# Later gathers, later output copies and no early matmuls in a four-layer routed transformer kernel

## The chip, the core and the metric

The kernel runs on one core of one Trainium2 chip. The metric is the device time of one launch in microseconds (us). The kernel before takes 969.09 us, the median of three runs (968.87 to 969.17).

## The reference

The input `x` holds 64 sequences of 64 tokens with 512 features, in float32. Four layers are added to it one after the other. Each sequence has its own indices, known only when the kernel runs.

```python
x = x + (einsum('bsi,bio->bso', x, W0[id]) + b0[id])           # id: one of 16 experts per sequence
x = x + (x @ W1.T + scale[a] * (x @ A[a].T) @ B[a].T)          # a: one of 7 adapters, rank 16
x = x + attention(x)                                            # 8 query heads, 4 key/value heads of 64
x = x + (einsum('bct,bcd->bdt', x, W3[subject]) + b3[subject])  # one of 8 matrices, 64 x 64
```

The attention layer makes q, k and v, normalises q and k, rotates them by their positions, writes k and v into a cache of blocks of 16 positions that a table of 257 entries per sequence addresses, and lets each token see the last 256 positions. So a sequence needs up to 255 old rows of the cache and its own 64 new ones, 320 positions in all.

## The kernel before, in words

A tile is 128 tokens, two sequences; there are 32 tiles. `x` lies transposed on the host (features on the partitions), so that the first matmul needs no transpose. All matmuls are in float32. The order of the instructions on every engine is written out by hand (`manual_schedule`): what is emitted first runs first on its engine, and the framework adds the semaphores.

**First part (0 to about 540 us): layers 0 and 1, and q, k, v.** Tiles go in groups of 1, 1, 2 and then seven times 4. For each group `layer1` does the matmuls of layer 1 (`pxa` L650, `p` L665, the adapter's L673), and while the next group's tiles come up, one turn of the loop does for tile `i0` of the next group and tile `i` of this one: `layer0(i0)` (L275, eight matmuls with two expert matrices that a DMA of 1 MB each brings), `load_next` (the loads two tiles ahead), `other` (index arithmetic on VectorE, copies of old cache rows), `turn_x2(i)` (four transposes L684), a q product and a k/v product (`product`, L140, four matmuls each), `turn0(i0)` (four transposes L298, then the addition L299 on VectorE), and `keep_kv(i)` (normalisation and rotation of k, then a store to the DRAM buffer `kvd`). When a group is followed by one twice as large (groups 1 to 2 and 2 to 4), each tile `i` has two turns, `half` 0 and 1, and its k/v product stands ahead of `turn0(i0)` in the second; in the groups of four it stands behind, inside the call of `keep_kv`. At the very start, two small helpers run matmuls of the identity with itself: `warm(3)` and `warm(6)` (L222), around the four matmuls `pb` that turn the biases.

**Second part (about 540 to 968 us): attention and layer 3, a loop of 32 steps.** Step `s` emits in this order:

- `load_kv(s + 2)`: five indirect DMAs (L801) on GpSimd's queue, 128 rows of 2 KB each, from `kvd` into the tile `kv` (four buffers, so tile `s + 2` takes the buffer of `s - 2`, which `attend(s - 2)` in step `s - 1` read last). In steps 0 and 1 a one-element copy on GpSimd, `after_keys`, holds them until the keys are turned. `load_mask(s + 2)` and `load_q(s + 2)` go to SP's queue.
- `scores(s)`: eight matmuls `ps` L874, one per key/value head and sequence; for each a fused add-and-maximum on VectorE (L882) and an exponential on ScalarE (L886) that also sums the row.
- `add_one(s - 2)`: an addition on GpSimd to layer 3's matrix (L847). `load_pair(s - 1)` goes to SP's queue.
- `attend(s - 1)`: 24 matmuls `po` L921 on the keys' values; then VectorE copies both results, `oT` L939.
- `normalise(s, 0)` and `normalise(s, 1)`: for each half a reciprocal L894 and four scalings L898 on VectorE.
- `last(s - 4)` in even steps from 4 on: layer 3 (`pz` L961), and the store of the output.
- `project(s - 2)`: eight records of `py` L949, then the addition L953 on VectorE.
- `keys(s + 1)`: ten transposes `pkt` (L855, L861), copied by ScalarE (L856, L862).
- `turn(s)`: 20 transposes `ppt` (L907, L911) of the normalised rows, copied to `pT` by VectorE and ScalarE in turn (L908, L912).

In steps 0 to 3 the q rows of the last tiles are still rotated on VectorE between these (`parts`). PSUM has eight banks. One belongs to `py`; the other seven are a ring, in which every new bank takes that of the seventh before it: `ppt` takes banks of `ps` and `po`, and `ps` takes those of `pkt` and `ppt`, once the copies have emptied them.

Of the kernel before, what the change touches and what calls it, by code (L numbers as in the profile page):

```python
# [12 lines left out]
F32 = mybir.dt.float32  # L13
I32 = mybir.dt.int32
AF = mybir.ActivationFunctionType
ALU = mybir.AluOpType
# [9 lines left out]
H, G, HD = 8, 4, 64  # L26
# [24 lines left out]
NT = NTOK // 128  # L51
# [8 lines left out]
def body(ctx: ExitStack, tc: tile.TileContext, a: dict, out: bass.AP):  # L60
    nc = tc.nc
    V, S, P, TE = nc.vector, nc.scalar, nc.gpsimd, nc.tensor
# [14 lines left out]
    ident = const.tile([128, 128], F32, name="ident")  # L77
# [21 lines left out]
    def bank(name):  # L99
        return ring.tile([128, 512], F32, tag="ring", name=name)  # L100
# [36 lines left out]
    def product(i, w, name, pool=None):  # L137
        ps = pool.tile([128, 512], F32, name="py") if pool else bank(name)
        for c in range(KC):
            TE.matmul(ps, x2s[i][:, c, :], w[:, c, :], start=c == 0, stop=c == KC - 1)  # L140
        return ps
# [43 lines left out]
    with ExitStack() as pa:  # L185
# [29 lines left out]
                ptok[h * B : (h + 1) * B, 4 * B : 4 * B + 1], tokf[:, 3, :], one[:, :1], start=True, stop=True  # L215
            )

        def warm(n):

            pw = bank("pw")  # L220
            for _ in range(n):
                TE.matmul(pw[:, :128], ident, ident, start=True, stop=True)  # L222

        toki = ptok[:, : 4 * B].rearrange("p (k b) -> p k b", k=4)

        warm(3)
        takes = su.tile([E, B], F32, name="takes")
        V.tensor_scalar(takes, toki[:E, 0, :], pidxf[:E], None, ALU.is_equal)
        biasT = su.tile([128, KC, B], F32, name="biasT")
# [1 line left out]
        for c in range(KC):  # L231
            TE.matmul(pb[:, c * B : (c + 1) * B], btab[:, c * 128 : (c + 1) * 128], takes, start=True, stop=True)
        V.tensor_copy(biasT.rearrange("p c b -> p (c b)"), pb[:, : KC * B])
        warm(6)
        kvi = su.tile([128, 1], I32, name="kvi")
        V.tensor_copy(kvi, ptok[:, 4 * B : 4 * B + 1])

# [65 lines left out]
        wkv = wts.tile([128, KC, D], F32, name="wkv")  # L303
# [384 lines left out]
        def keep_kv(i, pk, X):  # L688
            kvn = wk.tile([128, 2 * G * HD], F32, name="kvn", bufs=2)
            to = kvn[:, : G * HD].rearrange("p (h d) -> p h d", d=HD)  # L690
            run(turned(pk, G, to, wk, X, 1, *gains(1, i, wk, P)))
            S.copy(kvn[:, G * HD :], pk[:, G * HD :])
            nc.sync.dma_start(kvd[OLD + i * 128 : OLD + (i + 1) * 128], kvn)
# [38 lines left out]
        for g in range(NG - 1):  # L732
            layer1(tiles[g])
            if g == 0:
                scalars()
                turns[0] = rotation(0)
                for _ in range(4):
                    next(turns[0])
            elif g == 1:
                far()  # L740
            n, m = len(tiles[g]), len(tiles[g + 1])
            for k in range(m):

                i0, i, half, halves = tiles[g + 1][k], tiles[g][k * n // m], k % (m // n), m // n
                layer0(i0)
                load_next(i0)
                other(i0)
                if i0 % 4 == 1 and i0 // 4 + 1 < NT // 4:
                    load_a(i0 // 4 + 1)
                    load_b(i0 // 4 + 1)  # L750
                q = asked.pop() if asked and half == 0 else None
                if half == 0:
                    turn_x2(i)
                if q is not None:
                    pq = product(q, wq, "pq")
                pk = product(i, wkv, "pk") if half else None
                turn0(i0)
                if g == 0:
                    run(turns[0])
                    next(bg)  # L760
                    next(bg)
                if q is not None:
                    run(parts_q(q, pq, P))
                    made.append(q)
                if half == halves - 1:
                    keep_kv(i, pk if half else product(i, wkv, "pk"), P)
                    if i < NT - LATE:
                        asked.append(i)
                    if len(made) > 1:
                        turn_q(made.pop(0))  # L770
        layer1(tiles[-1])
        i = NT - LATE
# [19 lines left out]
    kvp = ctx.enter_context(tc.tile_pool(name="kvp", bufs=4))  # L792
    bp = ctx.enter_context(tc.tile_pool(name="bp", bufs=2))

    kvs, kTs, mbs, prs, pTs, oTs, qTs, pairs, x3s = {}, {}, {}, {}, {}, {}, {}, {}, {}

    def load_kv(i):
        kv = kvs[i] = kvp.tile([128, 5, 2 * G * HD], F32, name="kv")
        for n in range(5):
            at = idxn[:, n % 2, 2 * i + n // 2 :][:, :1] if n < 4 else idxh[:, i : i + 1]  # L800
            P.indirect_dma_start(  # L801
                out=kv[:, n, :], out_offset=None, in_=kvd,
                in_offset=bass.IndirectOffsetOnAxis(ap=at, axis=0),
            )

    def after_keys(i):

        seen = bp.tile([1, 1], F32, name="seen")
        P.tensor_copy(seen, kTs[i][0:1, 0, 0:1])

    def load_q(i, queue=nc.sync):
        qT = qTs[i] = bp.tile([128, 2, 2, 2, T], F32, name="qT", bufs=4)
# [51 lines left out]
    def scores(i):  # L864
        kT, mb, qT = kTs.pop(i), mbs.pop(i), qTs.pop(i)
        pr = bp.tile([128, G, 2 * NPOS], F32, name="pr")
        mx = bp.tile([128, G, 2], F32, name="mx")
        sm = bp.tile([128, G, 2], F32, name="sm")
        for gp in range(2):
            for b2 in range(2):  # L870
                ps = [bank("ps") for _ in range(2)]
                for g2 in range(2):
                    rows = slice(g2 * 64, (g2 + 1) * 64)
                    TE.matmul(  # L874
                        ps[g2][:, :NPOS], qT[rows, gp, b2].rearrange("p h t -> p (h t)"),
                        kT[rows, gp, b2 * NPOS : (b2 + 1) * NPOS], start=True, stop=True,
                    )

                for g2 in range(2):
                    g = 2 * gp + g2  # L880
                    p = pr[:, g, b2 * NPOS : (b2 + 1) * NPOS]
                    V.tensor_tensor_reduce(  # L882
                        out=p, in0=ps[g2][:, :NPOS], in1=mb[:, b2, :], scale=-1.0, scalar=3.0e38,
                        op0=ALU.add, op1=ALU.min, accum_out=mx[:, g, b2 : b2 + 1],
                    )
                    S.activation(  # L886
                        p, p, AF.Exp, bias=mx[:, g, b2 : b2 + 1], scale=-1.0, accum_out=sm[:, g, b2 : b2 + 1],
                    )
        prs[i] = (pr, sm)

# [23 lines left out]
    def attend(i):  # L914
        kv, pT = kvs.pop(i), pTs.pop(i)
        oT = oTs[i] = bp.tile([128, KC, 2, T], F32, name="oT")
        po = [bank("po") for _ in range(2)]

        def product(b2, g, rows, n, c, m, start, stop):
            gp, g2 = divmod(g, 2)  # L920
            TE.matmul(  # L921
                po[b2][g2 * 64 : (g2 + 1) * 64, gp * 128 : (gp + 1) * 128],
                kv[rows, n, (G + g) * HD : (G + g + 1) * HD], pT[rows, c, m * 128 : (m + 1) * 128],
                start=start, stop=stop,
            )

        for b2 in range(2):
            for gp in range(2):
                for c in range(2):
                    for g in (2 * gp, 2 * gp + 1):  # L930
                        n = 2 * b2 + c

                        product(b2, g, slice(0, 128), n, g, n, gp == 0 and c == 0, False)
        for gp in range(2):
            for b2 in range(2):
                for g in (2 * gp, 2 * gp + 1):
                    product(b2, g, slice(b2 * 64, (b2 + 1) * 64), 4, G, g, False, gp == 1)
        for b2 in range(2):
            V.tensor_copy(oT[:, :, b2, :], po[b2][:, :256].rearrange("p (k t) -> p k t", t=T))  # L939

# [67 lines left out]
    for s in range(NT):  # L1008
        if s + 2 < NT:
            if s < 2:  # L1010
                after_keys(s)
            load_kv(s + 2)
            load_mask(s + 2)
        if s and s + 2 < NT:
            load_q(s + 2)
        scores(s)
        if s >= 2:
            add_one(s - 2)
        if s:
            load_pair(s - 1)  # L1020
            attend(s - 1)
        else:

            parts[NT - 1] = parts_q(NT - 1, product(NT - 1, wq, "pq", pyp), V, cs[NT - 1])
            turn_q(NT - 3, bp)
        if s == 2:
            next(parts[NT - 1])
        normalise(s, 0)
        normalise(s, 1)
        if s % 2 == 0 and s >= 4:  # L1030
            last(s - 4)
        if s >= 2:
            project(s - 2)
        if s + 1 < NT:
            keys(s + 1)
        if s in (4, 5):
            turn_q(NT - 6 + s, bp)
        elif s in (2, 3):

            run(parts.pop(NT - 4 + s))  # L1040
        turn(s)
        if s == 0:
            load_q(2)
            nc.sync.dma_start(wo, a["woT"].rearrange("(c p) f -> p c f", p=128))
        elif s == 1:
            next(parts[NT - 1])
# [2 lines left out]
    add_one(i - 1)  # L1049
    add_one(i)  # L1050
    project(i - 1, ring=True)
    attend(i)
    last(i - 3)
    last_one(i - 1, 1)
    project(i, ring=True, parts=2)
# [54 lines left out]
```

## Time and profile before

| | us |
|---|---|
| median of three runs | 969.09 |
| the profiled run, device time | 969.89 |
| its span, first to last instruction | 967.9 |
| TensorE busy (PE) | 937.1, 97% |
| VectorE busy (DVE) | 609.0, 63% |
| ScalarE (ACT), GpSimd (POOL) busy | 405.0 and 402.6, 42% each |
| PE busy in 540 to 565, 565 to 578, 578 to 603 | 22.16, 9.20, 24.40 |
| PE busy in 603 to 910, 910 to 968 | 299.14, 54.39 |
| idle of GpSimd ahead of L801, waiting for `po` L921 | 155.8 |
| idle of VectorE ahead of `pT` L908, waiting for `ppt` L907 | 36.4 |

How to read it: the profile is that of one execution. Lines are those of the kernel before; PE is TensorE's matmuls and PEld its weight loads, which run beside them. A matmul's end is modelled, so a matmul that waits for a result can count as busy. The chain of waits goes back from the last instruction to what released it, step by step; a piece named PE is time in which TensorE's own work set the end. In the timeline the bracket at a row's end tells how long its engine stood idle before it and what ended that.

### The profile page before, as it was taken

The numbers are of one execution on the slowest core, as the hardware profiler recorded it, in microseconds if no ns is written. First come the engines' busy times: TensorE is split into PE (matmuls) and PEld (weight loads), VectorE is DVE, ScalarE is ACT, GpSimd is POOL, SyncE is SP. The second block draws the span as 40 slices with busy tenths as digits, with TensorE's granted clock in tenths as the row PEclk, the third lists the DMA queues.
The fourth block names the chain that finished last, engine by engine and source line by source line (L and its number), as shares of the span: only waits on it lengthen the run. The fifth ranks groups of instructions, "written<-read, shape, count | busy, mean of one in ns | idle before, by whom it ended". The sixth has DMA issues, their size and how long they took to land.

```text
span 967.9 us, 17834 instructions
## 1 busy us (share of the span) xinstructions
PE 937.1 (97%) x5425; PEld 513.4 (53%) x5425; DVE 609.0 (63%) x1734; ACT 405.0 (42%) x1081; POOL 402.6 (42%) x604
## 2 busy tenths in 40 slices
PE   8989999999999999999899979999999999999998
PEld 4434444444444444443344546766666666666665
DVE  4744776866976476442216868666767776667673
ACT  1312122322223222233223656656666666666663
POOL 4234355554553544534425543334444333334400
PEclk9989999999999999999999989999999999999999
DMA  8888999999999999999954774766666565666621
GB/s 303 301 291 293 397 397 332 374 375 367 381 335 389 401 339 385 354 362 380 350 217 142 237 254 135 213 206 204 205 197 194 182 193 180 201 197 201 200 68 45
DMA packets 132944, 260.74 MB, mean 269 GB/s; under 512 B 32481, under 2 KB 41186, under 8 KB 132850
## 3 DMA queue, kind: packets, MB, share of 16 engines
q1 hardware_dynamic: 108722, 178.74, 51.3%
q0 software_dynamic: 23232, 79.71, 24.8%
q10 hardware_dynamic: 896, 1.16, 0.3%
q8 instruction: 43, 0.70, 0.3%
q14 instruction: 51, 0.42, 0.1%
HBM read 190.06 MB, written 69.50 MB: 268 GB/s over the span
## 4 chain that ended last, share of the span: by engine, by line
PE 90%; DMA 4%; DVE 3%; SPq 1%; issue 1%; ACT 1%; DVEq 0%; ACTq 0%
PE py L949 12%; PE p L665 11%; PE pq L140 11%; PE p L275 10%; PE pk L140 10%; PE po L921 8%; PE ps L874 8%; PE ppt L907 6%; DMA w<-in_W 3%; PE pkt L855 2%; PE ppt L911 2%; PE px L684 1%; PE pkt L861 1%; PE pqt L174 1%; PE pz L961 1%; PE pt L298 1%
## 5 line engine op out<-in xcount | busy, mean ns | idle before, releaser
L801 POOL DMA_INDIRECT kv<-kvd,idxn x128 | 126.5, 988 | 212.8 <-PE po L921 155.8
L886 ACT ACTIVATE pr<-pr,mx 128x320 f32<-128x320 f32 x256 | 140.1, 550 | 7.2 <-DVE mx L882 3.2
L275 PE MATMUL p<-w,xt 128*64 128x512 f32 x512 | 120.4, 601 | 2.7 <-DMA w<-in_W 2.7
L949 PE MATMUL py<-wo,oT 128*128 128x512 f32 (+1 forms) x264 | 118.3, 591 | 1.7 <-DVE qn L128 1.7
L155 POOL DMA_INDIRECT st<-in_kvc,cidx x68 | 65.9, 970 | 125.1 <-DMA kvd<-st 107.8
L140 PE MATMUL pk<-wkv,x 128*128 128x512 f32 x256 | 115.6, 596 | 0.6 <-ACT x L686 0.6
L665 PE MATMUL p<-w,x 128*128 128x512 f32 x256 | 114.4, 603 | 0.0
L882 DVE CUSTOM_DVE_ANT_0 pr<-ps,mb 128x320 f32<-128x320 f32 x256 | 107.8, 485 | 6.2 <-PE ps L874 4.4
L140 PE MATMUL pq<-wq,x 128*128 128x512 f32 x248 | 111.3, 593 | 0.0
L874 PE MATMUL ps<-kT,qT 64*128 64x320 f32 x512 | 87.3, 460 | 10.8 <-DVE pT L908 6.8
L908 DVE COPY pT<-ppt 128x512 f32<-128x512 f32 x64 | 41.9, 687 | 74.3 <-PE ppt L907 36.4
L133 DVE TENSOR_TENSOR sq<-qn,sg 128x256 f32<-128x256 f32 (+1 forms) x128 | 40.1, 354 | 75.4 <-POOL sg L110 73.5
L898 DVE TENSOR_SCALAR pr<-pr,sm 128x320 f32<-128x320 f32 x256 | 85.2, 394 | 2.2
L921 PE MATMUL po<-pT,kv 128*64 128x128 f32 (+1 forms) x1536 | 84.3, 281 | 1.3 <-issue 1.3
L921 PEld LDWEIGHTS po<-pT,kv 128*64 128x64 f32 (+1 forms) x1536 | 70.5, 137 | 22.0 <-DVE mx L882 14.0
L123 ACT ACTIVATE ss<-ss,epst 128x4 f32<-128x4 f32 (+1 forms) x64 | 19.1, 299 | 146.7 <-DVE ss L122 136.5
L949 PEld LDWEIGHTS py<-wo,oT 128*128 128x128 f32 x264 | 47.5, 189 | 61.5 <-issue 58.4
L665 PEld LDWEIGHTS p<-w,x 128*128 128x128 f32 x256 | 48.3, 193 | 59.0 <-issue 57.2
L140 PEld LDWEIGHTS pk<-wkv,x 128*128 128x128 f32 x256 | 46.3, 190 | 51.1 <-issue 49.8
L275 PEld LDWEIGHTS p<-w,xt 128*64 128x64 f32 x512 | 35.3, 137 | 71.5 <-issue 64.8
L135 POOL TENSOR_TENSOR qr<-qn,sq 128x512 f32<-128x512 f32 x25 | 31.8, 1273 | 90.2 <-DVE qn L134 60.8
L140 PEld LDWEIGHTS pq<-wq,x 128*128 128x128 f32 x248 | 44.9, 190 | 46.2 <-issue 46.2
(202 smaller groups left out, 1336.5 us busy)
## 6 DMA issues: line engine op xcount, KB each, us to landing
w<-in_W SPq DMA_DIRECT2D x62, 1024.0 KB
kvd<-st SPq DMA_DIRECT2D x68, 512.0 KB
xt<-in_xT SPq DMA_DIRECT2D x32, 256.0 KB
x2d<-x2n SPq DMA_DIRECT2D x32, 256.0 KB
kvd<-kvn SPq DMA_DIRECT2D x32, 256.0 KB
qTd<-qTs SPq DMA_DIRECT2D x32, 256.0 KB
qT<-qTd SPq DMA_DIRECT2D x32, 256.0 KB
x2r<-x2d SPq DMA_DIRECT2D x32, 256.0 KB
```

Source lines behind the costliest of these rows:

```text
L140: TE.matmul(ps, x2s[i][:, c, :], w[:, c, :], start=c == 0, stop=c == KC - 1)
L155: P.indirect_dma_start(out=st, out_offset=None, in_=a["kvc"].rearrange("(n r) d -> n (r d)", r=2), in_offset=bass.IndirectOffsetOnAxis(ap= ...
L275: TE.matmul(p0[hs, :], xs[i][:, c, hs], w0s[i][h][:, c, :], start=c == 0, stop=c == KC - 1)
L665: TE.matmul(p1[i], x1s[i][:, c, :], w1[:, c, :], start=c == 0, stop=False)
L801: P.indirect_dma_start(out=kv[:, n, :], out_offset=None, in_=kvd, in_offset=bass.IndirectOffsetOnAxis(ap=at, axis=0),)
L874: TE.matmul(ps[g2][:, :NPOS], qT[rows, gp, b2].rearrange("p h t -> p (h t)"), kT[rows, gp, b2 * NPOS : (b2 + 1) * NPOS], start=True, stop= ...
L882: V.tensor_tensor_reduce(out=p, in0=ps[g2][:, :NPOS], in1=mb[:, b2, :], scale=-1.0, scalar=3.0e38, op0=ALU.add, op1=ALU.min, accum_out=mx[ ...
L886: S.activation(p, p, AF.Exp, bias=mx[:, g, b2 : b2 + 1], scale=-1.0, accum_out=sm[:, g, b2 : b2 + 1],)
L898: V.tensor_scalar(p, p, sm[:, g, b2 : b2 + 1], None, ALU.mult)
L907: TE.transpose(pt[:, n * 128 : (n + 1) * 128], pr[:, g, at : at + 128], ident)
L921: TE.matmul(po[b2][g2 * 64 : (g2 + 1) * 64, gp * 128 : (gp + 1) * 128], kv[rows, n, (G + g) * HD : (G + g + 1) * HD], pT[rows, c, m * 128 ...
L949: TE.matmul(py[:, fs], oT[:, c].rearrange("p b t -> p (b t)"), wo[:, c, fs], start=c == 0, stop=c == KC - 1,)
```

## The change

Four edits. `warm` and both its calls go. The k/v product of a tile moves behind `turn0` in the last turn of the two short groups (`k == m - 1`). In steps 2 to 29 `load_kv(s + 2)` moves behind `scores(s)`, and a one-element copy on GpSimd, `after_scores`, makes it wait for the fourth of the step's eight maxima; for that the maxima lie in two tiles, one for each half of the heads. And the copies `oT` leave `attend` for a function of their own, `keep_outputs`, which the loop calls behind `normalise`.

```diff
-        def warm(n):
-
-            pw = bank("pw")
-            for _ in range(n):
-                TE.matmul(pw[:, :128], ident, ident, start=True, stop=True)
...
-        warm(3)
...
-        warm(6)
...
-                pk = product(i, wkv, "pk") if half else None
+                pk = product(i, wkv, "pk") if half and k < m - 1 else None
                 turn0(i0)
...
-                    keep_kv(i, pk if half else product(i, wkv, "pk"), P)
+                    keep_kv(i, pk if half and k < m - 1 else product(i, wkv, "pk"), P)
...
+    def after_scores(i):
+
+        seen = bp.tile([1, 1], F32, name="seen")
+        P.tensor_copy(seen, mxs[i][0][0:1, 1, 1:2])
...
-        mx = bp.tile([128, G, 2], F32, name="mx")
+        mxs[i] = [bp.tile([128, 2, 2], F32, name=f"mx{gp}") for gp in range(2)]
...
-                        op0=ALU.add, op1=ALU.min, accum_out=mx[:, g, b2 : b2 + 1],
+                        op0=ALU.add, op1=ALU.min, accum_out=mxs[i][gp][:, g2, b2 : b2 + 1],
...
+        return oT, po
+
+    def keep_outputs(oT, po):
         for b2 in range(2):
             V.tensor_copy(oT[:, :, b2, :], po[b2][:, :256].rearrange("p (k t) -> p k t", t=T))
...
         if s + 2 < NT:
             if s < 2:
                 after_keys(s)
-            load_kv(s + 2)
+                load_kv(s + 2)
             load_mask(s + 2)
         if s and s + 2 < NT:
             load_q(s + 2)
         scores(s)
+        if 2 <= s < NT - 2:
+            after_scores(s)
+            load_kv(s + 2)
         if s >= 2:
             add_one(s - 2)
         if s:
             load_pair(s - 1)
-            attend(s - 1)
+            outs = attend(s - 1)
...
         normalise(s, 0)
         normalise(s, 1)
+        if s:
+            keep_outputs(*outs)
         if s % 2 == 0 and s >= 4:
             last(s - 4)
...
-    attend(i)
+    keep_outputs(*attend(i))
```

More of the change, by code (lines that the diff above doesn't have):

```diff
@@ L793, in body @@
     bp = ctx.enter_context(tc.tile_pool(name="bp", bufs=2))
-    kvs, kTs, mbs, prs, pTs, oTs, qTs, pairs, x3s = {}, {}, {}, {}, {}, {}, {}, {}, {}
+    kvs, kTs, mbs, prs, mxs, pTs, oTs, qTs, pairs, x3s = {}, {}, {}, {}, {}, {}, {}, {}, {}, {}
     def load_kv(i):
@@ L883, in scores @@
                         out=p, in0=ps[g2][:, :NPOS], in1=mb[:, b2, :], scale=-1.0, scalar=3.0e38,
-                        op0=ALU.add, op1=ALU.min, accum_out=mx[:, g, b2 : b2 + 1],
+                        op0=ALU.add, op1=ALU.min, accum_out=mxs[i][gp][:, g2, b2 : b2 + 1],
                     )
                     S.activation(
-                        p, p, AF.Exp, bias=mx[:, g, b2 : b2 + 1], scale=-1.0, accum_out=sm[:, g, b2 : b2 + 1],
+                        p, p, AF.Exp, bias=mxs[i][gp][:, g2, b2 : b2 + 1], scale=-1.0, accum_out=sm[:, g, b2 : b2 + 1],
                     )
```

## The prediction

> **What bounds the kernel now.** I read the page's busy times and chain first, then the chain of waits by stretches, then the timeline where the chain leaves TensorE.
>
> ```profile
> PE 937.1 (97%) x5425; PEld 513.4 (53%) x5425; DVE 609.0 (63%) x1734; ACT 405.0 (42%) x1081; POOL 402.6 (42%) x604
> PE 90%; DMA 4%; DVE 3%; SPq 1%; issue 1%; ACT 1%; DVEq 0%; ACTq 0%
> ```
>
> TensorE sets the time. A gain can come only from its holes and from matmuls counted busy while they wait. So I look for what one step of the second part costs with and without a hole. Chain of waits at 705 to 733 us (start, length, what), from the end of step 13 into step 14:
>
> ```profile
> 722.72 1.75 PE ppt L907 x16
> 724.47 0.99 PE ppt L911 x4
> 725.45 0.02 issue
> 725.48 0.70 DVE pT L908
> 726.18 0.04 issue
> 726.22 1.94 PE ps L874 x12
> ```
>
> The same chain at 905 to 950 us, end of step 29; no gather is left to issue there:
>
> ```profile
> 926.46 1.75 PE ppt L907 x16
> 928.21 0.44 PE ppt L911 x4
> 928.65 2.35 PE ps L874 x16
> ```
>
> Without the gathers the score matmuls follow the transposes at once. With them TensorE waits for the copy pT, which frees its PSUM banks. The timeline tells why the copy is late:
>
> ```profile
> 722.55 1.91 PE L907 MATMUL ppt<-ident,pr 128*128 128x128 f32 x16
> 723.49 0.94 POOL L801 DMA_INDIRECT kv<-kvd,idxh  x1 [0.31 <-issue]
> 725.48 1.29 DVE L908 COPY pT<-ppt 128x512 f32<-128x512 f32 x2 [3.12 <-PE ppt L911]
> ...
> 926.30 1.91 PE L907 MATMUL ppt<-ident,pr 128*128 128x128 f32 x16
> 926.94 0.69 DVE L908 COPY pT<-ppt 128x512 f32<-128x512 f32 x1 [0.84 <-PE ppt L907]
> ```
>
> The first four transposes of step 13 were done at 723.15, and VectorE stood idle until 725.48, 1.05 us after the fifth gather left GpSimd (723.49 + 0.94 = 724.43). In step 12 it is 1.08 us (711.73, 712.81), in step 27 1.03 us (915.53, 916.56); in step 29, without gathers, the copy starts 0.04 us after the fourth transpose. So TensorE's reports to VectorE and ScalarE are held back, from about 1.7 us before the fifth gather's end (L862 on ScalarE still started on time at 722.79) until some 1.05 us after it. Reports of VectorE to ScalarE and TensorE are not (L882 to L886 takes 0.04 us in such a stretch at 557).
>
> Price: L949 starts at 602.64 in step 4 and 909.96 in step 28, 307.32 us for 24 steps. The clean pair, 921.74 to 946.11, takes 24.37. Twelve such and two extra q transposes (0.44 each, steps 4 and 5) make 293.3. **14.0 us** are lost to this wait.
>
> The start of the second part has the second hole (chain, 500 to 605 us):
>
> ```profile
> 564.51 2.91 PE ps L874 x8
> 567.43 0.02 issue
> 567.45 0.59 ACT pT L908
> 568.04 0.04 issue
> 568.09 3.55 PE ps L874 x8
> 571.64 3.99 PE po L921 x48
> 575.63 0.02 issue
> 575.65 0.76 DVE oT L939 x2
> ```
>
> Here the fifth gather of kv(4) ends at 566.32; pT comes at 567.39, again 1.07 later. The granted clock is 0.50 from 567.8 to 574.7, and L949 waits for oT and qn until 577.29.
>
> **Part by part.**
>
> *Gathers after the fourth maximum.* Step 13 counts from its first score matmul, 713.05; its transposes L907 begin at +9.67 and the first bank is full at +10.1. Today the five gathers start when attend of that step ends: +5.3 to +11.4, reports free at +12.4. After: the fourth maximum is read at 715.73, +2.7; the small copy on GpSimd adds 0.34 (after_keys: 551.43 to 551.77), so gathers run from +3.1 to +9.2 (6.1 us as today) and reports are free at +10.25. That is just as the first bank fills, so pT is not late. What now falls into the held stretch (+7.5 to +10.25) is the end of L949 (+8.6) and of the key transposes (+8.9 to +9.7). If they all come at +10.25: L953 0.69, then both pT copies 1.29, end +12.3, and the next scores need the first at +12.5. ScalarE: three key copies 1.45, end +11.7, needed at +11.86; its three pT copies end at +13.3, needed at +13.6. No wait. Even steps have pz (0.86) ahead, so everything falls 0.86 later and outside. Behind the waiting copy on GpSimd stand the gathers and add_one; kv(s+2) is wanted by keys in the next step, 8 us after its last gather has landed (+12 or so), and add_one's w3 a step later: nobody waits. On SP nothing moves. Bounds: all 14.0 back, or a leftover of 0.3 per odd step (the spread of the release, up to 1.49 after the fifth gather). I take 1.0 left over: **-13.0**.
>
> *Outputs behind the normalisation.* L939, 0.76 us, waits 0.65 for po in each step; L894 and L898 go ahead of it by up to 1.3 us, held by the last exponential (+6.1). They end near +7.7 instead of +8.7, before L907 (+9.67) in either order. In odd steps the third and fourth ppt take po's banks and now need oT, done at +8.4: hidden. Alone worth 0 in a regular step, without gathers held too.
>
> *Steps 1 to 3.* kv(4) moves to step 2, kv(3) stays. Step 1: last maximum 560.1, eight L898 with two L894 2.9 to 563.0, oT to 563.6; ppt three and four wait for oT, so ppt ends at 564.6 (today 564.5). pT on both engines ends at 565.45 instead of 568.5; then ScalarE's sq 0.62, VectorE's L122 0.69, and the first L882 starts at 566.75 instead of 569.66. From there to the end of po: 4.1 us at full clock (1.58 as in step 3 and 2.50), 570.8; today 6.0. L949 needs qn after the eight L882 (3.3) and 0.9: 571.05 instead of 577.29. Step 2: L949 ends 574.7, kv(4)'s gathers end at 574.9, so L953 starts at 576.0; from it the first L882 of step 3 follows 4.0 later as today (581.03 to 585.04): 580.0 against 585.04. Step 3 has the same rotary work behind L953, may lose 0.6 or win 0.8. **-5.0**; -3.1 if the clock halves again, -5.8 if L953 isn't held.
>
> *No early matmuls.* Nine 128x128 matmuls of 0.42 go. The first weights are there at 6.5, and L275 starts only at 10.16 behind those matmuls; it can now start near 6.5, and its last part waits for the load of 11.98 (today it ends at 14.43). The end of the first part is not earlier for it: tile 1's weights land at 23.04 (chain: 14.14, 8.90 us of DMA), and TensorE waits for them today. The array works at half rate in this trace until about 11.7 (weight loads of L275 0.62 us apart, then 0.43). If it now stayed there until 22, L665 (3.6, from 17.0) and L673 would end near 24.1: +1.0. Between 0 and +1 I take **0**, the row of the DMA. [...]
>
> *Short groups.* Two products L140 (3.6 us each) move behind the four transposes L298: tiles 1 and 3. At 53.87 TensorE idles 3.56 us for L299, but VectorE is busy without a break from 45.96 (rotary work, then a run of L498 that stands ahead of L299), so TensorE's order changes nothing there. At the second place at most 0.3 idle: **0** (-0.3 to 0.1).
>
> Sum -18.0. The profiled run took 969.89 (span 967.9), so 951.9; the median of the runs is 0.8 lower: **951.1**.
>
> **Rivals.**
> 1. *A leftover in each odd step* (14%): the held stretch is longer in its new place and the key copies of ScalarE come late. Each 0.1 us costs 0.1 in twelve odd steps; with 0.5: 957.
> 2. *The delay doesn't come from the gathers* (7%): it stays with pT wherever they run. For it: mask, q and w3 loads also end with step 27. Against: the 1.03 to 1.08 above. Only the 1.7 us of 575.63 to 577.29 is won: 967.4, on the edge of what a measurement of this kernel tells from no change (0.2%, 1.9 us).
> 3. *Slower* (8%): gathers stretch where they now run, beside eight L882 and L898. The release moves with the fifth's end; key copies end 1.5 after it. With 1.4 us more in all an odd and its even step lose 1.6 and the gain of 18 is gone; with 2 us it is 975. The row: the third gather, beside L898, takes 1.08 instead of 0.95, so 0.13 each at most, 0.65 in all. [...]
> 4. *More* (5%): L953 isn't held, and the first part gains too: 947.
>
> **How the numbers follow.** The forecast has 66%, 948.5 to 954. The range leaves out the slower case and the unchanged delay: 947.5 to 961. Faster by over 0.2%: 66, 14, 5 and half of rival 2, 88%; within 4%; slower 8%.
>
> **What would show it.** Chain: 0.4 instead of 0.99 for L911 before each even step, no pT piece; L949 of steps 12 and 14 some 24.4 apart instead of 25.4. L801 starts 3 us after the first score matmul. L949 of step 2 starts 6 us earlier, without the half clock. Wrong if pT still starts 1 us after the fifth gather but with TensorE waiting, or if key copies end after the last transpose.

## The result, and the profile after

The changed kernel takes **974.56 us** (median of six runs, 973.11 to 978.15), the kernel before beside it 969.13 (968.81 to 970.87): a ratio of 1.0059 (95% interval 1.0037 to 1.0081). It is slower by 0.6%, where 951.1 was forecast. The profiled execution took 973.11 us, its span is 971.3. First the page of the changed kernel, busy times and chain:

```profile
PE 931.9 (96%) x5407; PEld 511.7 (53%) x5407; DVE 614.8 (63%) x1734; ACT 402.9 (41%) x1081; POOL 405.4 (42%) x632
PE 88%; DMA 3%; DVE 3%; issue 3%; SPq 2%; ACT 1%; another core or an unknown queue 0%; ACTq 0%; DVEq 0%
```

TensorE is busy 5.2 us less, and yet the span is 3.4 us longer: "issue", time for which the profile shows no cause, went from 1% of the chain to 3%. By stretches, cut where py L949 of a step starts (the first two columns are the profiled executions of before and after):

| stretch | before | after | difference |
|---|---|---|---|
| first part, up to the q product of tile 31 | 545.65 | 539.91 | -5.74 |
| start of the second part, to py of step 4 | 56.92 | 53.47 | -3.45 |
| 24 steps, py of step 4 to py of step 28 | 307.32 | 317.76 | +10.44 |
| from there to the end | 57.99 | 60.19 | +2.20 |

The 24 steps were to get 13 us shorter and got 10 longer. The last row has the same cause, since the gathers now run one step longer. The chain of the changed kernel over steps 13 and 14:

```profile
711.61 3.63 PE py L949 x8
...
716.44 0.19 issue
716.64 0.27 PE ppt L904
716.90 0.46 issue
...
725.23 3.63 PE py L949 x8
728.86 0.53 PE pkt L852 x4
729.39 0.89 issue
```

No piece is pT any more, and the score matmuls follow ppt at once, as forecast. But TensorE itself now stands still, 0.65 us in the middle of the transposes of step 13 and 0.89 in the key transposes of step 14, with nothing that it waits for. The timeline of step 13 tells more (start, length, engine, line; the bracket is the idle time ahead):

```profile
709.29 0.18 POOL L806 COPY seen<-mx 1x1 f32<-1x1 f32 x1 [6.00 <-DVE mx L879]
710.01 0.99 POOL L793 DMA_INDIRECT kv<-kvd,idxn  x1 [0.54 <-issue]
...
711.54 3.70 PE L949 MATMUL py<-wo,oT 128*128 128x512 f32 x8
...
715.06 0.95 POOL L793 DMA_INDIRECT kv<-kvd,idxh  x1 [0.30 <-issue]
...
717.46 0.76 DVE L939 COPY oT<-po 128x256 f32<-128x256 f32 x2 [3.23 <-PE pkt L858]
717.76 0.86 ACT L853 COPY kT<-pkt 128x384 f32<-128x384 f32 x2 [5.27 <-PE ppt L904]
```

po was done when py began, at 711.54. VectorE, free since 714.23, got to copy it only at 717.46, and ScalarE its first keys at 717.76, 1.4 and 1.7 us after the fifth gather's end (716.01). The name in the bracket is only that of the last semaphore. The trace also records each semaphore update. Counted by microsecond, those of TensorE and those of the DMA queues:

```
us from       708  709  710  711  712  713  714  715  716  717  718  719
TensorE         4    1    0    0    0    0    0    0    0    9    2    2
DMA queues     16   16   10    1    5    5    4    6    1    2   14   34
```

Between 709.13 and 717.43 not one report of TensorE went out, though po, py and three key banks were done in that time; then nine came within half a microsecond. Those of the DMA queues trickle. VectorE, ScalarE and GpSimd report as ever: each of their updates between 600 and 930 us stands within 0.02 us of the end of an instruction.

### The profile page after: what moved, and what is told of

Read it like the earlier page. It is cut to its first block, busy times and chain, and to the rows that moved or that the text cites. A ratio compares the mean times of both kernels' runs of the same rounds, so it can differ in the third digit from the quotient of the medians.

```text
span 971.3 us, 17756 instructions
## 1 busy us (share of the span) xinstructions
PE 931.9 (96%) x5407; PEld 511.7 (53%) x5407; DVE 614.8 (63%) x1734; ACT 402.9 (41%) x1081; POOL 405.4 (42%) x632
## 4 chain that ended last, share of the span: by engine, by line
PE 88%; DMA 3%; DVE 3%; issue 3%; SPq 2%; ACT 1%; another core or an unknown queue 0%; ACTq 0%; DVEq 0%
PE py L949 12%; PE p L657 11%; PE pq L140 11%; PE p L267 10%; PE pk L140 10%; PE ps L871 8%; PE po L918 8%; PE ppt L904 6%; DMA w<-in_W 3%; PE pkt L852 2%; PE pkt L858 2%; PE px L676 1%; PE pqt L174 1%; PE ppt L908 1%; PE pt L290 1%
## 5 line engine op out<-in xcount | busy, mean ns | idle before, releaser
L793 POOL DMA_INDIRECT kv<-kvd,idxn x128 | 126.1, 985 | 51.8 <-issue 45.4
L949 PE MATMUL py<-wo,oT 128*128 128x512 f32 (+1 forms) x264 | 118.6, 592 | 0.8 <-issue 0.8
L895 DVE TENSOR_SCALAR pr<-pr,sm 128x320 f32<-128x320 f32 x256 | 88.8, 408 | 2.3
L871 PE MATMUL ps<-kT,qT 64*128 64x320 f32 x512 | 82.3, 445 | 2.6 <-DVE pT L905 1.5
L949 PEld LDWEIGHTS py<-wo,oT 128*128 128x128 f32 x264 | 47.5, 189 | 61.3 <-issue 60.1
L806 POOL COPY seen<-mx 1x1 f32<-1x1 f32 x28 | 5.0, 177 | 175.3 <-DVE mx L879 175.3
L291 DVE TENSOR_TENSOR x<-pt,x 128x512 f32<-128x512 f32 x32 | 22.1, 689 | 85.4 <-PE pt L290 72.8
L939 DVE COPY oT<-po 128x256 f32<-128x256 f32 x64 | 24.8, 419 | 79.5 <-PE pkt L858 28.2
L904 PE MATMUL ppt<-ident,pr 128*128 128x128 f32 x512 | 66.0, 275 | 9.0 <-issue 6.6
```

Of the source, the lines that this page charges most:

```text
L793: P.indirect_dma_start(out=kv[:, n, :], out_offset=None, in_=kvd, in_offset=bass.IndirectOffsetOnAxis(ap=at, axis=0),)
L871: TE.matmul(ps[g2][:, :NPOS], qT[rows, gp, b2].rearrange("p h t -> p (h t)"), kT[rows, gp, b2 * NPOS : (b2 + 1) * NPOS], start=True, stop= ...
L895: V.tensor_scalar(p, p, sm[:, g, b2 : b2 + 1], None, ALU.mult)
L904: TE.transpose(pt[:, n * 128 : (n + 1) * 128], pr[:, g, at : at + 128], ident)
L949: TE.matmul(py[:, fs], oT[:, c].rearrange("p b t -> p (b t)"), wo[:, c, fs], start=c == 0, stop=c == KC - 1,)
```

## The experiments

Runs of one group ran on one chip, with the kernel before beside them. "Start" and "24 steps" are the second and third stretch above, from each run's own profile.

| run | us | ratio to before (95% interval) | start | 24 steps |
|---|---|---|---|---|
| group 1, before 973.59: a_first | 972.43 | 0.9997 (0.9973 to 1.0020) | 57.6 | 309.8 |
| b_gathers | 1032.80 | 1.0576 (1.0528 to 1.0624) | 64.6 | 361.7 |
| c_outputs | 969.93 | 0.9967 (0.9945 to 0.9989) | 56.5 | 308.9 |
| f_direct | 949.09 | 0.9747 (0.9724 to 0.9769) | 50.1 | 293.3 |
| group 2, before 947.89: g_max1 | 945.59 | 0.9973 (0.9959 to 0.9988) | 47.8 | 293.3 |
| g_max2 | 946.83 | 0.9991 (0.9972 to 1.0009) | 47.9 | 293.3 |
| g_max8 | 945.85 | 0.9984 (0.9966 to 1.0003) | 47.9 | 293.3 |
| h_three | 945.15 | 0.9973 (0.9955 to 0.9991) | 47.6 | 293.3 |
| group 3, before 969.89: after_again | 976.43 | 1.0071 (1.0045 to 1.0097) | 54.0 | 315.6 |
| g_max1_again | 1069.07 | 1.1027 (1.0988 to 1.1067) | 56.5 | 403.2 |
| g_max2_again | 1039.38 | 1.0650 (1.0561 to 1.0739) | 57.6 | 373.8 |
| g_max8_again | 965.19 | 0.9955 (0.9926 to 0.9983) | 51.8 | 311.2 |
| group 4, before 972.86: n_bufs3 | 970.01 | 0.9967 (0.9946 to 0.9988) | 55.3 | 307.7 |
| h_three_again | 949.17 | 0.9749 (0.9718 to 0.9781) | 50.5 | 293.3 |
| f_pool | 947.94 | 0.9745 (0.9710 to 0.9780) | 50.5 | 293.3 |
| group 5, before 974.60: s14_max4 | 950.43 | 0.9741 (0.9715 to 0.9767) | 49.9 | 293.3 |
| s14_max2 | 949.07 | 0.9723 (0.9690 to 0.9756) | 49.9 | 293.3 |
| group 6, before 975.06: s14_early | 952.83 | 0.9774 (0.9749 to 0.9798) | 50.7 | 293.3 |

### Group 1: which edit does it, and is it the gathers?

**a_first** undoes the gathers' and the outputs' move; only the first part is changed.

> Only the edits of the first part (no early matmuls, short groups reordered); the loop of the second part as before. After reached L140 of tile 31, the start of the second part, 5.7 us earlier than before (539.98 against 545.72). Theory 1, the edits do this: 963.4 us. Rival, most of it is the half clock of 55.83 to 62.65, which costs 3.4 us and may come back: 966 to 967. Rival as predicted (0): 969.

The ratio is 1 within 0.3%. The 5.7 us that the changed kernel's profile shows in the first part are no effect of the edits: in the 18 profiles of kernels with this first part the second part starts anywhere from 539.9 to 549.3, 545.1 in the median; the one profile of before has 545.65.

**b_gathers** puts the copies back ahead of the normalisation (first diff), **c_outputs** the gathers back to the head of the step (second).

```diff
-            outs = attend(s - 1)
+            keep_outputs(*attend(s - 1))
...
-        if s:
-            keep_outputs(*outs)
```

```diff
-                load_kv(s + 2)
+            load_kv(s + 2)
...
-        if 2 <= s < NT - 2:
-            after_scores(s)
-            load_kv(s + 2)
```

> The changed kernel with the outputs copied where the kernel before copies them, ahead of the normalisation; the gathers stay held to the fourth maximum. Theory 1, the gathers hold back TensorE's reports through almost their whole run, po's among them (released 5.8 us late in step 13): VectorE now stands at that copy ahead of the ten instructions of the normalisation (2.9 us), so the transposes come up to 2.9 us later in each of 27 steps: 990 to 1050 us. Rival 2, the moved copies do the harm, since they keep po's banks from ppt: without the move the gathers bring what was predicted, 951 to 957.

> The changed kernel with the gathers back at the head of the step (no wait for a maximum, the maxima still in two tiles); the outputs stay behind the normalisation. Theory 1: the move alone costs nothing, as the first part alone gives: within 2 us of the run with the first part only, 962 to 965. Rival 2, the moved copies do the harm: 972 to 976.

b_gathers is 59 us slower than before. VectorE's timeline in one step of it:

```profile
719.21 0.76 DVE L939 COPY oT<-po 128x256 f32<-128x256 f32 x2 [6.65 <-PE pkt L858]
719.88 0.17 DVE L891 RECIPROCAL sm<-sm 128x4 f32<-128x4 f32 x1
```

VectorE stands 6.65 us at the copy until 1.4 us after the train of gathers (711.77 to 717.77) has ended, and the normalisation queues behind it. So the moved copies are not the culprit: with the gathers held to the fourth maximum they save some 50 us (a ratio of 1.0059 with the move against 1.0576 without it, on different chips). With the gathers where they were (c_outputs) they change the 24 steps by 0.9 us; that run was expected within 2 us of a_first and lies 2.5 below it.

**f_direct** loads as many bytes without GpSimd.

```diff
+            if i >= 4:
+                nc.sync.dma_start(kv[:, n, :], kvd[n * 128 : (n + 1) * 128, :])
+                continue
```

> The changed kernel, in which from tile 4 on the five gathers of a step are plain loads of the same size on SP's queue (128 fixed rows each, so the values are not the reference's); they too wait for the fourth maximum, by a load of one element on that queue. Theory 1, what holds the reports back is GpSimd's issuing of the gathers, not their data: every pair of steps takes some 24.4 us, 398.5 us of the loop become about 368: 944 us. Rival 3, the data of the loads collide with TensorE's reports wherever they are issued: 965 to 975.

The 24 steps take 293.29 us, 11.75 and 12.61 in turn. So the held reports come from the gathers on GpSimd, not from their bytes, and the clean step is what the prediction took it for (293.3).

### Groups 2 and 3: another point to hold the gathers to

The maxima get eight tiles of their own, and `seen` reads the first, second or eighth:

```diff
-        P.tensor_copy(seen, mxs[i][0][0:1, 1, 1:2])
+        P.tensor_copy(seen, mxs[i][1][0:1])
```

> The changed kernel with the gathers held to the first maximum of the step in place of the fourth (the eight maxima lie in tiles of their own). Theory 1: TensorE's reports are held from some 0.7 us after the first gather's start to some 1.2 us after the fifth's end, and only what falls behind the end of that stretch is paid for. The train starts 1.2 us earlier, its end lies ahead of the key transposes, and the last score matmul just escapes it: 948 to 955 us. If the last score matmuls fall into it, each step pays several us: over 1000. Rival 2, any wait of the gathers inside the step costs as the fourth maximum does: 970 to 978.

> As the run before, but held to the second maximum, 0.8 us earlier than the fourth. Theory 1: the stretch of held reports ends 0.8 us earlier in every step, TensorE no longer stalls, a rest of some 0.3 us is left in odd steps: 950 to 960 us. Rival 2: 970 to 978.

> As the run before, but held to the eighth maximum, 1.6 us later than the fourth. Theory 1: po's report goes out ahead of the gathers, and the stretch ends about 12.4 us after the first score matmul, where it ends in the kernel before; the copies pT are late as they are there: 962 to 972 us, no worse than the fourth maximum. Rival 2, the later the wait the more it costs: 990 and more.

> The changed kernel in which two of the five gathers of tiles 4 and up are plain loads of the same size on SP's queue (fixed rows, so the values are not the reference's); the other three stay held to the fourth maximum. Theory 1: the stretch is as long as the train of gathers, so it ends 2.5 us earlier, ahead of the key transposes, and every step is clean: 944 to 949 us. Rival, the stretch has a length of its own (about 8 us, whatever runs in it): 965 to 975.

These four told nothing apart, because on this chip no report is held, nor, to judge by its time of 947.89 us, in the kernel before. The gathers take as long (g_max2, one step: 700.82 to 706.92), but from 701 to 707 the DMA queues record 96 updates, where the changed kernel had 31 between 710 and 716, and po's report goes out in the middle, at 703.24, when it is due. The other groups were run on five other chips, where the kernel before takes 969.9 to 975.1. Three of the four once more on one of those, with the changed kernel beside them:

> The changed kernel itself once more, beside the runs that follow and on their chip. On the chip of the run f_direct the kernel before took 973.6 us and lost 13 to 15 us to held reports; on the chip of the runs g_max1 to h_three it took 947.9 and no report was held, so nothing could be told apart there. If this chip holds reports: before 967 to 975, the change 1.003 to 1.008 of it. If it doesn't: before 946 to 950, the change 0.997 to 1.000 of it, since only the start of the second part is left to gain.

> First maximum. If this chip holds reports, theory 1 (the stretch goes from some 0.7 us after the first gather's start to some 1.2 us after the fifth's end, and what counts is where its end falls): 948 to 957 us, or over 1000 if the last score matmuls fall into it; rival 2 (any wait inside the step costs as the fourth maximum does): 970 to 978. If it doesn't hold them: 944 to 948, as on the chip before.

> Second maximum. If this chip holds reports, theory 1: 950 to 960 us, rival 2: 970 to 978. If it doesn't: 944 to 948.

> Eighth maximum. If this chip holds reports, theory 1: the stretch ends where it ends in the kernel before, 962 to 972 us; rival 2: 990 and more. If it doesn't: 944 to 948.

My theory was wrong about the early side: the first maximum costs 99 us and the second 69, where 948 to 960 was expected. The escape that the expectation left, over 1000 if the last score matmuls are caught, doesn't apply: the last of the eight fused additions on VectorE, which waits for them, starts 1.6 to 1.7 us after the first gather in every step of g_max1_again and 1.2 us after it in g_max2_again, so they were not held. Only the eighth came out as expected. The timeline of g_max2_again shows why (gathers from 706.12 to 712.23):

```profile
705.97 2.55 PE L918 MATMUL po<-pT,kv 128*64 128x128 f32 x44
708.87 0.27 PE L918 MATMUL po<-pT,kv 64*64 64x128 f32 x1 [0.35 <-issue]
...
710.41 0.30 PE L918 MATMUL po<-pT,kv 64*64 64x128 f32 x1 [0.43 <-issue]
711.83 6.52 PE L949 MATMUL py<-wo,oT 128*128 128x512 f32 x8 [1.12 <-issue]
```

TensorE stops within po, whose last four matmuls wait for nobody, and starts py 1.12 us after them, while GpSimd still issues. So the train doesn't only keep TensorE's reports, it also stops TensorE, and the more so the earlier it starts: of the chain of the 24 steps "issue" is some 46 us with the first maximum, 33 with the second, 14 with the fourth (the changed kernel), 0.7 with the eighth and in the kernel before. What stops it no run here shows. At the first stop above, 708.52, one report was due and unsent, that of po's first half.

Part of the loss is a second effect. py takes 6.52 us here, where 3.70 is usual, largely because TensorE's granted clock is halved (start and end, length, busy us of PE, PEld, VectorE, ScalarE and GpSimd, granted clock, DMA share, GB/s):

```profile
710.93:717.74 6.81, 5.91 (x7) 2.48 (x8) 0.94 (x3) 0.00 (x0) 1.33 (x3) 0.50 0.75 233
```

Over the 24 steps of g_max1_again, g_max2_again and b_gathers the clock is halved for 34 to 41 us, which costs at most half of that, 17 to 20 us, of the 68 to 110 that these steps lose against clean ones. In the 24 steps of the changed kernel, of g_max8_again and of the kernel before it never falls.

### Group 4: the length of the train, the kind of load, and a wait for po

**h_three** (again) leaves three gathers to GpSimd and gives two to SP's queue. **f_pool** is f_direct with the loads on GpSimd's queue. **n_bufs3** moves `load_kv(s + 2)` behind `attend(s - 1)` and takes three kv buffers in place of four, so that the gathers wait for po.

> Three gathers by GpSimd behind the fourth maximum, two of the five as plain loads of fixed rows (values not the reference's). If this chip holds reports, theory 1 (the stretch is as long as the train of gathers): it ends some 1.2 us after the third, 2.5 us earlier than with five; TensorE is nearly clean, 944 to 952 us. Rival (a stretch with a length of its own, some 8 us): 965 to 975. If it holds none: 944 to 948.

> The changed kernel with the gathers of tiles 4 and up as plain loads of 128 fixed rows, on GpSimd's queue and behind the fourth maximum (values not the reference's). If this chip holds reports: where the index lists do it, 944 to 950 us; where every load that GpSimd issues does it, 965 to 985. If it holds none: 944 to 948.

> The changed kernel without the wait for the maximum: the gathers of tile s + 2 stand behind attend(s - 1) and take the buffer that it reads (three buffers in place of four), so they start once po's report is out, as in the kernel before, but the first two of them no longer collide with the start of the second part. If this chip holds reports: the 24 steps from 4 to 28 take 307 to 310 us, as in the kernel before (307.3), and the start of the second part (from the q product of tile 31 to py of step 4) 50 to 53 instead of 57: ratio 0.990 to 0.996 of the kernel before. Rival: the wait for po costs as much as that for a maximum, over 1.003. If it holds none: 0.996 to 0.999.

With three gathers TensorE's silence is 5.6 us in place of 8.3 (it still ends 0.7 to 1.1 after the last gather) and every step is clean. Five plain loads by GpSimd take it 2.76 us in all (714.49 to 717.25 in one step), with no silence but what the work has by itself: po is done at 716.09 and its report goes out at 716.12, where with three gathers po's report, due 1.3 to 1.4 us after the first of them starts, goes out 4.4 to 4.7 us after it. So it is the gathers with index lists that do it, not every load that GpSimd issues. Whether the list itself does it, or rows that lie apart in DRAM, these runs don't tell, since each plain load reads 128 rows in one block. n_bufs3 has the steps of the kernel before (307.7) and gains 1.6 us at the start, less than was expected (55.3 against 50 to 53); its ratio, 0.9967, is as good as c_outputs.

### Groups 5 and 6: a version that uses it

If only the length of each train between two needed reports counts, five gathers can be split: one behind a maximum, whose silence ends ahead of po's report, and four behind po, which end 1.25 us earlier than five would. The kv tile becomes two, one with four buffers and one with three:

```diff
+        if part != 1:
+            kvs[i] = [kvp.tile([128, 2 * G * HD], F32, name="kv0", bufs=4)]
+        if part:
+            kv4 = kvp.tile([128, 4, 2 * G * HD], F32, name="kv4", bufs=3)
...
             after_scores(s)
-            load_kv(s + 2)
+            load_kv(s + 2, 0)
...
             outs = attend(s - 1)
+            if s + 2 < NT:
+                load_kv(s + 2, 1)
```

> The changed kernel with the train split: one gather behind the fourth maximum, the other four behind attend(s - 1), released by po's report (their buffers, three in place of four, are those that it reads). Theory 1 on a chip that holds reports: the single gather's stretch ends about when po's report is due; the four end 1.25 us earlier than five do in the kernel before, so pT in odd steps is late by at most 0.3 us; 24 steps in 293 to 300 us instead of 307 to 310, and the start of the run n_bufs3 or better: ratio 0.975 to 0.985 of the kernel before, 948 to 958 us. Rival (two trains cost as much as one long one): 24 steps in 305 to 312, ratio 0.99 to 1.00. On a chip that holds none: 944 to 948 us.

> As the run before, with the single gather behind the second maximum, 0.8 us earlier: its stretch may catch the last two score matmuls, but ends ahead of po's report. Theory 1 on a chip that holds reports: within 0.5% of the run before, better where po's report was late there; over 975 where the last score matmuls are caught in every step. On a chip that holds none: 944 to 948 us.

Both take 0.97 of the kernel before, a little less than was expected, and their 24 steps are clean. One step of s14_max4:

```profile
706.95 0.98 POOL L797 DMA_INDIRECT kv<-kvd,idxn  x1 [0.48 <-DMA qT<-qTd]
...
708.79 1.11 POOL L797 DMA_INDIRECT kv<-kvd,idxn  x1 [0.51 <-PE po L922]
...
712.80 0.95 POOL L797 DMA_INDIRECT kv<-kvd,idxh  x1 [0.30 <-issue]
...
714.57 1.29 DVE L909 COPY pT<-ppt 128x512 f32<-128x512 f32 x2 [1.80 <-PE ppt L908]
...
715.24 1.92 PEld L875 LDWEIGHTS ps<-kT,qT 64*128 64x128 f32 x16 [0.17 <-issue]
```

pT is still late, 0.82 us after the last gather's end, but the transposes are not done before 715.3, and the score matmuls start at once: 1.25 us less of train is just enough.

**s14_early** puts the nine early matmuls back into s14_max2, since in 13 of the 18 profiles without them the mean granted clock of the first 40 us was 0.91 or 0.96 (its rows begin only at 10 to 15 us).

> The run s14_max2 with the nine early matmuls put back. In the 18 profiles without them, the mean granted clock of the first 40 us is 1.00 in five, 0.96 in nine and 0.91 in four, and the second part starts at 543.3, 545.3 and 547.9 us on average; in the one profile with them (the kernel before) it is 1.00. Theory A, the early matmuls keep the clock up: 1.00 in the first 40 us, second part from 541 to 545, and a ratio 0.002 to 0.005 below that of s14_max2 on a chip that holds reports: 0.967 to 0.971. Theory B, the clock of the first 40 us has nothing to do with them: 0.91 or 0.96 again in most executions, ratio 0.972 to 0.975. On a chip that holds no reports the two give 0.993 to 0.995 and 0.996 to 0.999.

The clock was 0.96 with them too (0.70 from 15 to 20 us), and the ratio is not lower, 0.9774 against 0.9723, on different chips. Theory A falls: in this profile they didn't keep the clock up, and their removal costs nothing that can be seen. Theory B's range for the ratio, 0.972 to 0.975, was missed as well.

## Why the prediction was wrong, point by point

- **The price of the stall: right.** 293.3 us for 24 clean steps were predicted, 293.29 to 293.32 measured in every run whose steps are clean, and 14.0 us to be won. That the gathers cause it was right too (f_direct); rival 2, a delay that doesn't come from them, is out.
- **The step that failed: where the held stretch begins.** The prediction read its start off step 13, "about 1.7 us before the fifth gather's end", and moved it along with the train's end. In the kernel before, the reading is right: py is done at 721.62 and the last key bank at 722.72, 3.3 and 4.4 us after the first gather's start, and those who wait for py and the key banks start at once:

```profile
717.92 3.70 PE L949 MATMUL py<-wo,oT 128*128 128x512 f32 x8
...
718.33 0.96 POOL L801 DMA_INDIRECT kv<-kvd,idxn  x1 [6.25 <-PE po L921]
...
721.66 0.69 DVE L953 TENSOR_TENSOR x<-py,x2r 128x512 f32<-128x512 f32 x1
...
722.05 0.86 ACT L856 COPY kT<-pkt 128x384 f32<-128x384 f32 x2 [2.98 <-PE pkt L855]
...
722.79 0.61 ACT L862 COPY kT<-pkt 128x512 f32<-128x512 f32 x1
```

But the stretch doesn't keep that start when the train moves. In the changed kernel po's report was due at 711.61, 1.6 us after the first gather's start, and went out at 717.43. So what falls into the stretch is oT, pz, py and the key banks, and not just the end of py and of the key transposes, and the -13.0 us of the forecast became +10.4 over the 24 steps. The profile of before could not show this: in its odd steps TensorE has nothing to report from 0.3 us before the first gather's start to 3.3 us after it, and that is where po's report lies after the change. Why reports due 3.3 to 4.4 us into the train pass there, while here one due at 1.6 and those behind it are held to the end, no run shows. Rival 1 named a longer stretch, but counted only late key copies, up to 957 us.

- **The end of the stretch: mis-sized by 0.7 us.** +10.25 was forecast, from the first score matmul; it was +10.9 (706.49 to 717.43). The first gather starts 0.72 us after the small copy does (709.29 to 710.01), where 0.34 was taken, and the release comes 1.4 us after the fifth gather, where 1.05 was.
- **That TensorE stops itself** wasn't thought of: 0.65 and 0.89 us in the pair shown above, most of the 1.83 us by which this pair of steps (py at 699.03 to 725.23, 26.20) is longer than a clean one (24.37). Over the 24 steps it is 14 of the 24.5 us that they lose against clean ones; the rest is mainly the late copies oT (some 2 us of the chain) and longer pieces of the key transposes and of ppt (some 4 and 2).
- **Slower by rival 3? No.** The sign is its, the mechanism is not: the five gathers take 5.99 us in the step shown and at most 6.2 in 23 of the 24 (7.03 in step 5, where 1.24 us pass between the second and the third), where 6.1 was usual before.
- **Outputs behind the normalisation: 0, right** with the gathers where they were (308.9 against 309.8). But with the gathers held they are what keeps the change from costing 59 us.
- **Start of the second part: mis-sized.** 5.0 predicted, 3.45 measured here and 2.95 in after_again. py of step 2 does start 7.1 us earlier, reckoned from the q product of tile 31 (24.6 against 31.6; 6.2 was forecast), without the half clock, and py of step 3 still 5.0 earlier, as forecast for that step. The term that was wrong is the next interval, to py of step 4: it gives 1.5 of this back (15.04 us against 13.52), where a loss of 0.6 at most was taken. Most of the gathers of kv(5), 577.1 to 583.2, fall into it. On the chip that holds no reports the whole stretch takes 47.6 to 47.9.
- **No early matmuls, short groups: 0, right** (a_first: -2.6 to +1.9 us). A half clock that the kernel before has at 55.83 stayed away in the changed kernel's profile, but came at 56.66 in that of after_again; it is no effect of the edits.

What stays open: why one chip of six holds no reports, what in a gather holds them on the others, and what sets where in the train the hold on TensorE begins. No run here shows on which core of its chip it ran.

## What to carry to other kernels

When a report is late near some engine's work, count the semaphore updates over the whole stretch of that work: a report that is not due can't be seen to be late, so the trace shows a hold only where a report is due. Before work with such a shadow is moved, lay the full length of that work over the new place, and not only the part that was seen to hold, and list every report due in it. If it is too long for any gap, split it by the gaps: one gather ahead of po's report and four behind it are 0.974 of the kernel before, all five together 1.006 at one place and 1.10 at another.

## What the hardware did that I had not expected

- While GpSimd issued gathers by index lists back to back, semaphore updates of TensorE and of the DMA queues were held; those of VectorE, ScalarE and GpSimd were not (each within 0.02 us of an instruction's end). With five gathers TensorE was silent for 8.3 us in the median step of the changed kernel. In 18 of its 24 steps TensorE's first report went out 1.0 to 1.5 us after the fifth gather's end; in five, one or two went out alone, up to 1.8 us ahead of that end, and in step 5 reports went out in the pause of 1.24 us between the second gather and the third. With three gathers the silence was 5.6 us, until 0.7 to 1.1 after the last. The DMA queues recorded 31 updates in the 6 us of the changed kernel's train, and 96 where nothing was held (g_max2). With five plain loads by GpSimd po's report, due at 716.09, went out at 716.12.
- Where in the train the hold on TensorE begins differs: a report due 1.3 to 1.6 us after the first gather's start was held in the changed kernel, while in step 13 of the kernel before those due 3.3 to 4.4 us after it went out on time.
- In such a stretch TensorE stopped, 0.19 to 1.12 us at a time in the rows above, with no wait that the profile shows: first 2.4 us after the first gather's start in the step of g_max2_again, 6.4 us after it in step 13 of the changed kernel.
- Whether this happens differed between the six chips on which groups of runs were made: on five the kernel before takes 969.9 to 975.1 us, on the sixth, where no report was held, 947.9.
- The first part, the same in 18 profiles of kernels on several chips, ends up to 9 us apart (539.9 to 549.3 us), so a gain there can't be read from one profile.
